# An attention kernel on TensorE: softmax sums over 8 rows with shared rows added by VectorE, outputs divided by GpSimd, fewer score columns, and layer 0's queries turned by VectorE

## The chip, the cores and the metric

The kernel runs on one core of a Trainium2 chip. The metric is the device time of one execution in microseconds (us). The five engines that matter are TensorE (PE; its weight loads are listed apart as PEld), VectorE (DVE), ScalarE (ACT), GpSimd (POOL) and SyncE (SP), which issues the transfers.

## The reference

The input `x` is 16 images of 64 x 64 positions with 256 channels, in float32. Two residual layers follow each other. Each starts with a group norm over 32 groups (`gn`, eps 1e-5, no scale or shift) and has 8 heads of 32.

```
# layer 0: linear attention over the n = 4096 positions of an image
q, k, v = split(gn(x) @ w_qkv)                # 8 heads x 32
q = softmax(q, over the 32 of a head) * 32**-0.5
k = softmax(k, over the 4096 positions)
context = einsum('bhdn,bhen->bhde', k, v)
x = x + einsum('bhde,bhdn->bhen', context, q) @ w_out

# layer 1: attention of each position to its 7 x 7 neighbours, zeros around the image
q, k, v = gn(x) @ Wq + bq, gn(x) @ Wk + bk, gn(x) @ Wv + bv
kp, vp = unfold(k, 7), unfold(v, 7)           # 49 neighbours of each position
kp = kp + e       # emb0 by row for heads 0 to 3, emb1 by column for heads 4 to 7
attn = softmax(einsum('bhwnd,bhwndk->bhwnk', q, kp), over the 49)
x = x + einsum('bhwndk,bhwnk->bhwnd', vp, attn)
```

## The kernel before

**Layout.** An image lies in SBUF as two tiles of 128 channels x 4096 positions, `img[k]`, each held twice, since the next image is loaded and normalised while the present one is worked on. The 4096 positions are in block order: 8 strips of 512, and a strip is a vertical stripe of 8 columns by 64 rows (strip 0 is made of the 3 columns at the left edge and the 5 at the right). `ORDER`, `KEYED` and `UNITS` are orders over strips and over units of the attention. `qq` (128 x 2 x 4096) holds layer 0's queries first and layer 1's later. PSUM has eight banks: `double` is two pairs (in the trace `pd`), `single` four banks (`ps`); `psum2()` takes the pairs by turns, `banks()` goes round all four pairs of banks.

**Order of the work.** For PE, ACT, DVE and SP the order of instructions is the order in which the code is written (`manual_schedule(engines=ORDERED)`); only POOL's is left to a scheduler. Semaphores make an engine wait for what it reads, and for the readers of a buffer that it overwrites. Everything runs image by image.

**Layer 0.** `layer0` has a loop of 16 steps of 256 positions. In a step, L524 makes queries and keys of two blocks of 128 positions on TensorE (positions on the partitions, 512 columns), L528 takes the exponential on ACT, L531 and L533 form the sums and reciprocals over a head on VectorE, L534 multiplies the queries by them on GpSimd. L542 adds the previous step's keys, times the input with a column of ones (257 columns), into two PSUM banks that stay open for the whole loop. `transposed` turns the queries of the step before that: four transposes by the identity on TensorE (L556) into one bank, and one copy of 512 columns into `qq`, by ACT in odd steps (L560) and by VectorE in even ones (L562). L284 normalises the strip that comes next. After the loop, `cc` holds the two halves of the normalised context, and `output_weights` (L302 to L324) turns them, multiplies them by the value weights, masks what belongs to other heads, and multiplies by `w_out`, into `w2`: one 256 x 256 matrix for the image. The output stage then takes, for each strip, four matmuls 128 x 128 x 512 of `w2` with `qq` (L602), and VectorE adds them to the image (L611) and takes the statistics for layer 1's group norm (L460).

**Layer 1, before the attention.** `positional` makes the scores of each query with the position embedding (L644, evacuated by L633 on ACT and L635 on VectorE), which go to DRAM and come back as 32 extra rows of `qq` (`store_rings`, `load_rings`); rows of masks stand beside the keys in `kaug` to match, so that one matmul of 64 rows gives key and embedding scores and a large negative number outside the 7 x 7. `values` (L692) makes the values and stores them padded to DRAM; `keys_queries` (L720) makes keys and queries for one half of the heads. The weights `wq`, `wk` and `wv` lie in SBUF as read, and are scaled into second tiles for each image.

**The attention.** `local_attention` runs twice per image, for half 0 (heads 0 to 3, `hg` = 0) and half 1. Each goes through four units of 16 columns of the image, each unit through 9 chunks `c` of 8 key rows, taken in five groups `g` of two (the last has one). The queries that see a chunk lie in the rows `lo` to `hi` of `span(c)`: 14 rows, or 8 at the top and 10 at the bottom. For each chunk and each of two planes `pl`:

- `scores` (L782): keys on the partitions, queries in the columns, into a pair of banks `pd`. The 128 partitions are two blocks `e` of 8 columns of keys. A block is reached by queries of 16 columns from up to three key strips, and the matmuls per row of queries take 10, 16 and 6 columns.
- ACT takes the exponential of all of them (L790) into a work tile `e`.
- `weighted` (L813), one group later (`held`): for each 8 columns `j` and each of 4 heads, one matmul with the values adds the weighted sum into `outs[j]`, and one with a matrix of ones adds the softmax's sum into `zs[j]`. All chunks of a unit add up in these four banks, which L800 fills with zeros first (`zb`, four matmuls with bf16 operands), since each adds only to the rows `lo` to `hi`.
- `finish`, after the last group of a unit: VectorE turns `zs` (L826), ACT copies `outs` out of PSUM (L827), VectorE copies the one column that matters, takes the reciprocal, turns it back to all rows (L831 to L833) and multiplies the outputs by it (L837); GpSimd adds them to the image (L846). The tiles for this come from a pool `tail` with two buffers.
- `between` puts other work between the groups: loads and statistics of the next image, its group norm, and the stores of what is done (`store_out`).

A matrix multiplication in float32 is recorded as two TensorE records for each instruction. A second, general path for inputs whose sums leave the safe range follows the fast one in the program; a flag `ok` skips it, and with these inputs it does not run.

## Time and profile before

| what | value |
|---|---|
| median of 3 runs | 5968.38 us (5966.06 to 5989.82) |
| profiled execution | 5964.21 us, of which the profile's span is 5962.4 us |
| mean granted TensorE clock in the span | 0.973 |
| busy share of the span | PE 92%, PEld 62%, DVE 49%, ACT 38%, POOL 17% |
| scores (L782) | 27648 records, 1012.9 us busy |
| products with values and with ones (L813) | 18432 records each, 841.1 and 839.4 us busy |
| exponentials (L790) | 1152, mean 839 ns |
| transposes of layer 0's queries (L556) | 1024 records, 151.0 us busy |
| transfers | 526.94 MB, 88 GB/s on average |

A row of the groups names the line, the engine, the operation, what it writes and reads (partitions x elements) and how often it ran; then the busy time and the mean of one in ns; then how long the engine was idle just before, and what ended most of that. In the table above a row can mix shapes; the shapes apart are shown where they are used. The chain of waits goes back from the last instruction, from each step to what released it or to the one before it on its engine; "issue" in it is time in which the engine waited for nothing that the profile shows.

### The profile page before, as it was taken

To read this page: it belongs to the slowest core of one execution; us is meant where nothing else is said; L and a number is where in the kernel's file an instruction comes from. 1 tells how busy PE (TensorE), PEld (TensorE's weight loads), DVE (VectorE), ACT (ScalarE), POOL (GpSimd) and SP (SyncE) were. 2 spreads that over 40 slices of the span, in tenths; PEclk is the share of its full clock that TensorE was granted. 3 is DMA by queue.
4 is the path that set the end of the run, shared out by engine and by line. 5 is a ranking of instruction groups with operands and counts; after the bars stand their busy time and mean duration, and the time that the engine had idled before them with its cause. 6 is when DMAs were issued, how large, how long until landed. Compare 5 with 4: busy or idle time off the path is not lost.

```text
span 5962.4 us, 171738 instructions
## 1 busy us (share of the span) xinstructions
PE 5478.6 (92%) x76913; PEld 3722.9 (62%) x76913; DVE 2892.6 (49%) x5034; ACT 2253.0 (38%) x3233; POOL 1029.1 (17%) x1944
## 2 busy tenths in 40 slices
PE   7999899998989989999899998999989999899998
PEld 4665666656666565665656656566565665656656
DVE  4544445554455544455445454444544545445454
ACT  1441523425244252442524425244252433515334
POOL 3021120211202012020121201212022120221202
PEclk9999999999999999999999999999999999999999
DMA  4543615435154361644516345073450724517244
GB/s 117 112 98 54 119 52 107 103 64 111 49 115 95 68 118 38 119 96 77 105 38 126 91 74 112 31 130 87 74 116 29 139 76 75 115 33 144 66 77 84
DMA packets 736939, 526.94 MB, mean 88 GB/s; under 512 B 240432, under 2 KB 667696, under 8 KB 733744
## 3 DMA queue, kind: packets, MB, share of 16 engines
q1 hardware_dynamic: 736192, 515.86, 42.6%
q8 instruction: 605, 9.91, 0.7%
q14 instruction: 142, 1.16, 0.1%
HBM read 357.02 MB, written 158.73 MB: 86 GB/s over the span
## 4 chain that ended last, share of the span: by engine, by line
PE 87%; ACT 4%; issue 4%; DVE 2%; SPq 1%; DMA 1%; POOL 1%; ACTq 0%; DVEq 0%; POOLq 0%
PE ps L813 16%; PE pd L782 15%; PE pd L524 14%; PE pd L720 7%; PE ps L542 7%; PE ps L720 6%; ACT qq L633 4%; PE ps L602 4%; PE pd L602 4%; PE ps L692 4%; PE pd L692 4%; PE ps L644 2%; PE ps L556 2%; PE ps L800 1%; SPq L504 0%
## 5 line engine op out<-in xcount | busy, mean ns | idle before, releaser
L790 ACT ACTIVATE e<-pd 128x896 f32<-128x896 f32 (+2 forms) x1152 | 924.2, 839 | 1039.7 <-PE pd L782 1037.8
L782 PE MATMUL pd<-qq,kaug 64*64 64x140 f32 (+5 forms) x27648 | 1012.9, 287 | 158.3 <-ACT qq L633 77.8
L782 PEld LDWEIGHTS pd<-qq,kaug 64*64 64x64 f32 x27648 | 891.3, 136 | 314.4 <-issue 170.6
L524 PE MATMUL pd<-wqkv,img 128*128 128x512 f32 x2048 | 922.2, 594 | 3.1 <-DVE img L284 3.1
L813 PE MATMUL ps<-e,ones 128*32 128x112 f32 (+1 forms) x18432 | 839.4, 253 | 65.2 <-issue 65.1
L813 PE MATMUL ps<-e,vw 128*32 128x112 f32 (+1 forms) x18432 | 841.1, 256 | 59.6 <-issue 59.2
L826 DVE STREAM_TRANSPOSE r<-ps 128x512 f32<-128x512 f32 x256 | 168.9, 697 | 1267.1 <-PE ps L813 1267.1
L438 POOL TENSOR_TENSOR others<-others,rc 128x16 f32<-128x16 f32 x256 | 113.5, 443 | 2961.3 <-DVE rc L831 2917.1
L528 ACT ACTIVATE eq<-pd 128x1024 f32<-128x1024 f32 x256 | 262.2, 1024 | 953.3 <-PE pd L524 953.3
L813 PEld LDWEIGHTS ps<-e,vw 128*32 128x32 f32 x18432 | 495.7, 111 | 202.8 <-issue 164.2
L633 ACT ACTIVATE qq<-ps,bias 32x512 f32<-32x512 f32 (+2 forms) x544 | 321.1, 623 | 781.0 <-PE ps L644 716.7
L524 PEld LDWEIGHTS pd<-wqkv,img 128*128 128x128 f32 x2048 | 372.4, 191 | 381.1 <-issue 352.4
L813 PEld LDWEIGHTS ps<-e,ones 128*32 128x32 f32 x18432 | 539.6, 112 | 76.4 <-issue 75.8
L531 DVE TENSOR_REDUCE qz<-eq 128x16 f32<-128x512 f32 x256 | 175.5, 686 | 829.2 <-ACT eq L528 829.2
L542 PE MATMUL ps<-xtok,eq 128*128 128x257 f32 x2048 | 486.1, 380 | 0.0
L542 PEld LDWEIGHTS ps<-xtok,eq 128*128 128x128 f32 x2048 | 386.1, 190 | 149.0 <-issue 107.1
L846 POOL TENSOR_TENSOR img<-img,r 128x320 f32<-128x320 f32 (+1 forms) x512 | 419.4, 840 | 165.3 <-DVE rc L831 164.1
L633 ACT ACTIVATE kaug<-pd,bias 32x512 f32<-32x512 f32 x256 | 173.9, 679 | 633.8 <-PE pd L720 630.9
L635 DVE TENSOR_SCALAR qq<-ps,bias 32x512 f32<-32x512 f32 x384 | 309.9, 807 | 146.8 <-PE ps L720 141.1
L460 DVE BATCH_NORM_STATS2 st<-img 128x6 f32<-128x512 f32 x512 | 334.9, 684 | 13.8 <-DMA img<-in_xc 5.1
L534 POOL TENSOR_TENSOR eq<-eq,qr 128x512 f32<-128x512 f32 x256 | 275.0, 1074 | 30.6 <-DVE qr L533 1.7
L720 PE MATMUL ps<-img,wqn 128*128 128x512 f32 x512 | 250.6, 635 | 0.0
(125 smaller groups left out, 6176.4 us busy)
## 6 DMA issues: line engine op xcount, KB each, us to landing
vw<-vpad SPq DMA_DIRECT2D x512, 288.0 KB
img<-in_xc SPq DMA_DIRECT2D x256, 256.0 KB
xtok<-in_xt SPq DMA_DIRECT2D x64, 1024.0 KB
out<-img SPq DMA_DIRECT2D x256, 256.0 KB
vpad<-v SPq DMA_DIRECT2D x112, 512.0 KB
qq<-pos SPq DMA_DIRECT2D x128, 256.0 KB
qq<-in_ring SPq DMA_DIRECT2D x128, 256.0 KB
pos<-qq SPq DMA_DIRECT2D x128, 112.0 KB
```

Of the source, the lines that this page charges most:

```text
L460: nc.vector.bn_stats(st[:, k, s], x[k][:, strip(s)])
L524: nc.tensor.matmul(ps[:, t], xn[k][:, n0 : n0 + P], n.wqkv_sb[:, k, : 2 * C], start=(k == 0), stop=(k == 1))
L542: nc.tensor.matmul(pc[hg][:, : C + 1], eq[p][:, t, C + hg * P : C + (hg + 1) * P], xtok[p // 4][:, 2 * (p % 4) + t], start=(p == 0 and t = ...
L602: nc.tensor.matmul(py[co], w2[:, hg, co * P : (co + 1) * P], qq[:, hg, strip(s)], start=(hg == 0), stop=(hg == 1),)
L633: nc.scalar.activation(dst, src, AF.Identity, bias=bias)
L635: nc.vector.tensor_scalar(dst, src, bias, None, ALU.add)
L692: nc.tensor.matmul(pi[:, t], x[k][:, n0 : n0 + P], wv[:, k], start=(k == 0), stop=(k == 1))
L720: nc.tensor.matmul(ps[a], wgt[:, k, hg * P : (hg + 1) * P], x[k][:, strip(pair[a])], start=(k == 0), stop=(k == 1),)
L782: nc.tensor.matmul(to, kaug[pl][rows, u, 8 * c : 8 * c + 8].rearrange("p r w -> p (r w)"), q, start=True, stop=True,)
L790: nc.scalar.activation(e, ps[:, :, : 2 * m], AF.Exp)
L813: nc.tensor.matmul(dst, ones if to is zs[j] else vw[:, j, c, h * HD : (h + 1) * HD], pr, start=False, stop=(c == NB - 1),)
L846: nc.gpsimd.tensor_tensor(yv, xv, by_rows(add[:, :, a - w0 : e - w0], xv), ALU.add)
```

## The change

1. **Queries of layer 0.** `transposed` becomes `turned`: two VectorE instructions per step transpose each 32 x 32 block of 128 x 256 within its partitions, straight from the work tile into `qq`. The queries lie differently then: partition 32a + d holds dimension d of every head, at the positions 32a to 32a + 31 of each block of 128. No transpose on TensorE and no copy is left.
2. **Output of layer 0.** To match, the output weights are kept per head on each of four groups of 32 rows (`w4`, in a buffer of the window pool). They are made by four transposes, 16 matmuls with 32 columns of weights, a scaling, eight matmuls with 32 rows, and three copies. The output stage takes, for two strips at a time, matmuls of 32 rows, 128 columns of weights and 256 columns of queries, adding over 8 heads, for four groups of rows `a`: 256 matmuls an image, where there were 32. VectorE adds the results to the image in 4 pieces of 256 for the first 128 channels and 2 of 512 for the second.
3. **Score columns.** The pieces of a row of 16 queries are 8, 14 and 6 columns instead of 10, 16 and 6. What is no longer written in `pd` is set to a large negative number once per half (`nb` times `bits`), and in half 1 the scores are laid out with a constant pitch of 16 rows so that these places stay the same for every chunk.
4. **Sums.** A row of queries reaches two chunks at 6 of 8 rows. `both_chunks` adds the 6 shared rows of the chunk before into this chunk's exponentials, in place, on VectorE. `summed` then multiplies by ones only the 8 rows that are complete after chunk `c`, for 16 columns at once, into their own columns of `zs`. The eight matmuls per chunk with ones (4 heads by two groups of 8 columns, over 14 rows) are replaced by four over 8 rows and 16 columns, or by eight over 6 and 2 rows where these lie on both sides of the border between the two banks of `zs`. The sums come one group after the products (`late`).
5. **Division.** `finish` is a generator of three parts, of which one runs per group. GpSimd multiplies the outputs by the turned reciprocals and then adds them to the image. The pool `tail` has one buffer for each of its two tags, `work` has six instead of four. The stores (`store_out`) are issued after the part with GpSimd.
6. **Weights.** `wq`, `wk` and `wv` have one tile each; SP loads them again for every image and VectorE scales them in place. `ORDER` changes so that pairs of strips stand together.

```diff
-ORDER = (3, 4, 5, 6, 7, 1, 2, 0)
+ORDER = (4, 5, 6, 7, 0, 1, 2, 3)
...
-        work = ctx.enter_context(tc.tile_pool(name="work", bufs=4))
-        tail = ctx.enter_context(tc.tile_pool(name="tail", bufs=2))
+        work = ctx.enter_context(tc.tile_pool(name="work", bufs=6))
+        tail = ctx.enter_context(tc.tile_pool(name="tail", bufs=1))
...
-            def transposed(p):
-                pt = other[p % 2]
+            def turned(p):
+
                 e = eq.pop(p)
...
+                for t in range(2):
+                    T = 2 * p + t
+                    nc.vector.transpose(qv[:, :, HD * T : HD * T + HD], e[:, t, :C].rearrange("p (h d) -> p h d", d=HD))
...
+            w4 = window(f"w4_{b}")[:, : 8 * C].rearrange("p (h g c) -> p h g c", h=4, g=2)
+            for h in range(2):
+                nc.vector.tensor_copy(w4[:, h].rearrange("p g c -> p (g c)"), double[0][:, h])
+            nc.scalar.copy(w4[:, 2:4].rearrange("p h g c -> p h (g c)"), double[1])
...
+            for i in range(NS // 2):
+                s0 = ORDER[2 * i]
...
                 for co in range(2):
...
+                    py = [double[a // 2][:, a % 2, : 2 * P] if co else single[a][:, : 2 * P] for a in range(4)]
+                    for h in range(4):
+                        for hg in range(2):
+                            for a in range(4):
+                                rows = slice(HD * a, HD * a + HD)
+                                nc.tensor.matmul(
+                                    py[a],
+                                    w4[rows, h, hg, co * P : (co + 1) * P],
+                                    qv[rows, 4 * hg + h, 8 * HD * i : 8 * HD * (i + 1)],
+                                    start=(h == 0 and hg == 0),
+                                    stop=(h == 3 and hg == 1),
+                                )
...
+        def load_weights(to, name):
+            nc.sync.dma_start(to, io[name].rearrange("(k p) f -> p k f", p=P))
...
-                    for e, u, w0, w1 in ((0, 2 * t, 0, 10), (1, 2 * t + 1, 0, 16), (0, 2 * t + 2, 10, 16)):
+                    for e, u, w0, w1 in ((0, 2 * t, 0, 8), (1, 2 * t + 1, 2, 16), (0, 2 * t + 2, 10, 16)):
...
+            def both_chunks(c, e, before):
+
+                r0 = 8 * c - 2 * PAD
+                part = rows_of(c, e, r0, 8 * c)
+                nc.vector.tensor_tensor(part, part, rows_of(c - 1, before, r0, 8 * c), ALU.add)
...
+            def summed(c, e):
...
+                r0, r1 = max(8 * c - 2 * PAD, 0), min(8 * c + 8 - 2 * PAD, W)
+                for i in range(2):
+                    a, z = max(r0, 32 * i), min(r1, 32 * i + 32)
+                    for h in range(4 if a < z else 0):
...
+                        nc.tensor.matmul(dst, ones, pr, start=True, stop=True)
...
+            def finish(i, t, r, pvs):
+
+                for k in range(2):
+
+
+                    nc.vector.transpose(r[:, k], zs[k])
+                yield
...
+                nc.vector.tensor_tensor(rc[:, 0], turned[:, :, 0], turned[:, :, 0], ALU.max)
+                nc.vector.reciprocal(rc[:, 1], rc[:, 0])
+                nc.vector.transpose(turned, rc[:, 1].unsqueeze(2).to_broadcast([P, 32, HD]))
+                yield
...
-                    nc.vector.tensor_tensor(pv, pv, r[j][:, 0], ALU.mult)
...
+                    nc.gpsimd.tensor_tensor(pv, pv, rz, ALU.mult)
...
+                stored(i)
+                yield
...
                 if held:
                     i, g, es = held
                     for c, e in es:
-                        weighted(UNITS[i], c, e, vw[i])
+                        weighted(c, e, vw[i])
                     if g == 4:
+                        rs[i] = [tail.tile([P, 2, 512], F32, tag=f"tail{k}", name=f"r{b}_{hg}_{i}_{k}") for k in range(2)]
+                        for j in range(2):
+                            nc.scalar.copy(rs[i][1][:, j], outs[j])
...
+                if late:
+                    i, g, es = late
+                    for c, e in es:
+                        summed(c, e)
+                    if g == 4:
+                        ends.append(finish(i, UNITS[i], *rs.pop(i)))
+                if held:
+                    for c, e in held[2]:
+                        if c:
+                            both_chunks(c, e, before)
+                        before = e
+                for end in list(ends):
+                    if next(end, True):
+                        ends.remove(end)
+                if late:
+                    between(*late[:2])
+                held, late = new, held
```

## The prediction

> **What bounds the kernel now.** I read the page from the top: busy shares, then the chain that ended last.

> ```profile
> PE 5478.6 (92%) x76913; PEld 3722.9 (62%) x76913; DVE 2892.6 (49%) x5034; ACT 2253.0 (38%) x3233; POOL 1029.1 (17%) x1944
> PE 87%; ACT 4%; issue 4%; DVE 2%; SPq 1%; DMA 1%; POOL 1%; ACTq 0%; DVEq 0%; POOLq 0%
> ```

> TensorE is 87% of the chain, so a tensor cycle removed is time unless something else takes its place. Taking each stage from the first record of its first line, an image (median of 16) is: queries and keys of layer 0 95.2 us, output of layer 0 33.1, positional 10.3, values 29.5, keys and queries 27.0, attention of half 0 73.5, keys and queries 26.5, attention of half 1 73.2. Both attentions are 40% of the span. Next the chain in order of time, inside an attention (start, us, what) and inside the loop of layer 0:

> ```profile
> 2478.95 1.68 PE pd L782 x37
> 2480.63 0.33 PE ps L800 x4
> 2480.95 1.36 PE ps L813 x64
> 2482.31 1.68 PE pd L782 x37
> 2483.99 1.28 PE ps L813 x47
> 2485.27 2.82 issue
> 2488.09 0.64 PE ps L813 x17
> ...
> 2338.36 3.44 PE pd L524 x8
> 2341.80 1.74 PE ps L542 x8
> 2343.54 0.44 PE ps L556 x4
> ```

> In attention scores (L782) and products (L813) alternate without a wait on ACT. Two chunks of 14 rows cost 1.68 us of scores and 1.67 of products; a unit of 9 chunks comes to 13.9 us. But units 1 and 2 of a half take 17.9 us from L800 to L800 on average: 4 us are lost. The "issue" piece is the largest part: TensorE stops in mid-group with no semaphore, and in the trace a 16 KB transfer of the instruction queue lands about 1 us before it resumes. Such gaps come to some 220 us over the run. The rest is half clock (mean granted clock 0.973).

> Then the groups by shape:

> ```profile
> L782 PE MATMUL pd<-qq,kaug 64*64 64x224 f32 x7168 | 833.7, 367 | 24.0 <-issue 24.0
> L813 PE MATMUL ps<-e,ones 128*32 128x112 f32 x14336 | 715.9, 265 | 62.0 <-issue 62.0
> L556 PE MATMUL ps<-ident,eq 128*128 128x128 f32 x1024 | 151.0, 273 | 0.0
> L800 PE MATMUL ps<-zb 32*128 32x512 bf16 x512 | 62.3, 384 | 48.2 <-ACT qq L633 48.1
> L837 DVE TENSOR_TENSOR r<-r 128x512 f32<-128x512 f32 x256 | 221.4, 865 | 28.2 <-DVE r L833 1.4 <-ACT eq L528 0.5
> L833 DVE STREAM_TRANSPOSE r<-rc 128x512 f32<-128x512 f32 x256 | 182.1, 711 | 8.8
> L534 POOL TENSOR_TENSOR eq<-eq,qr 128x512 f32<-128x512 f32 x256 | 275.0, 1074 | 30.6 <-DVE qr L533 1.7
> L846 POOL TENSOR_TENSOR img<-img,r 128x320 f32<-128x320 f32 x256 | 253.2, 989 | 165.3 <-DVE rc L831 164.1 <-DVE r L837 1.3
> L846 POOL TENSOR_TENSOR img<-img,r 128x192 f32<-128x192 f32 x256 | 177.0, 692 | 0.0
> ```

> The means of matmuls are latencies; their cost is the pitch. Start to start, the four column tiles of L813 take 42.6 ns a round at 48 columns and 56 at 64: 0.833 ns a column and 2.7 ns, per record. Each matmul is two records.

> [...] L837 takes 691 ns alone and up to 1256 when an L846 is running, starting its own work when that ends. [...] L800 is that shape: its four records start within 10 ns and the group costs 0.33 us, so here they do overlap, but in bf16 and one round only.

> **The change part by part**, against the profiled execution's 5964.2 us (span 5962.4 and 1.8 around it).

> 1. *Queries turned by VectorE.* L556 goes: 0.44 us in each of 16 steps of 16 images, less what the tail gives back. The tail from the last L542 to the first output matmul is now 6.8 us; the new one has the two cc steps 1.3, two scalings 0.9, 32 records in column tiles 1.0, a scaling 0.4, 16 row-tiled records 1.0, the first copy of w4 0.7 and handovers, some 6.5. Sum -110 us. Added on VectorE: two transposes of 256 a step. The 512 row is 711; half of it is the floor, 711 the ceiling; I take 0.43 each. With L531 0.69, L533 0.25 and L284 0.85 a step asks 2.65 us of VectorE under 5.17 of TensorE, so it is hidden (3.2 at the ceiling).

> 2. *Output of layer 0.* 32 matmuls of 512 columns become 256 of 256 with 32 rows, four abreast: 512 records, 128 rounds of 256 x 0.833 + 2.7 = 216 ns = 27.6 us against 28.0. Nothing, if they overlap. [...] The last evacuation grows from 0.70+0.69 to 2 x 0.69 + 2 x 0.68 = 2.75: +1.4 us on the path, +22. Its other VectorE work is 5.8 us per pair of strips under 6.9 of TensorE.

> 3. *Fewer score columns.* Each quadrant of the array streams 28 columns per row of queries instead of 32: 112 rows x 4 x 2 records x 0.833 = -0.75 us a unit, -96 over 128 units.

> 4. *Sums over 8 rows.* Before, 36 rounds of ones per unit: 28 x 96 + 4 x 56 + 4 x 43 = 3.08 us. After, 20: twelve of 128 columns at 109, four of 96 at 83, four of 32 at 29 = 1.76. -1.32 us a unit, -169. The score buffers' fill adds 0.33 a half, +11.

> 5. *Added waits.* The shared rows are added in place by VectorE, eight of 384 per unit at 0.56, or 0.4 behind a GpSimd instruction plus the wait for it. Each waits for the products that read the tile, and the sums, two steps behind the scores, wait for it; about 2.8 us of TensorE work lies between, so it is covered except at a half's last unit, where no scores follow: +0.8 us, +26. The multiply moves to GpSimd, and tail has one buffer per tag now: the ACT copy of a unit's outputs waits until GpSimd has finished the unit before. Behind that copy stand the next exponentials on ACT and the next unit's products on TensorE. The loop from copy to copy: two copies 1.2; next unit's first products, last sums, a group of scores and its products 3.5; VectorE's last addition, maximum, reciprocal (0.35 for 32) and transpose of 1024 (1.25) 2.6; GpSimd two multiplies 2.1 and adds 3.0 (half 1, where L846 runs at 1.15 and 0.74: 3.8); five additions of VectorE that exclude it 2.0: 14.4 us in half 0, 15.2 in half 1. TensorE's own unit is now 13.9 - 2.07 = 11.8, and with the 4 us lost today 15.8. So the loop is just covered while the losses stay outside it. Bounds for units 1 and 2 of each half: nothing, or losses fully on top of the loop, 15.0 + 4 - 15.8 = 3.2 us. I take 0.6: 64 x 0.6 = +38.

> 6. *At nothing:* SP gets four weight loads an image (0.9 MB of 33), needed a stage later; stores now wait on SP for GpSimd, and behind them stands a window load wanted one unit later. If that cover went, a late window stops products, as in 5. The end of the program gains a multiply, +2.

> Sum: -110 + 22 - 96 - 169 + 11 + 26 + 38 + 2 = -276: 5688, and since the median of the runs lies 4 us above the profiled execution, **5690**.

> **Rivals.** *The loop binds.* For it: 15 us is more than TensorE's 11.8, and instruction gaps fell 6 us after a unit's end, where the loop's TensorE part lies. [...] Losses on top: (3.2 - 0.6) x 64 = +166: 5856. *Row tiles don't overlap* (the slower side): if the 128-column weights of the four row tiles load one after another at L556's 110 ns, a record costs 110 instead of 54 ns: 512 x 56 = +28.7 us an image, +459: about 6150. It decides above 89 ns a record (276/16/512 = 34 ns more than 54). For it: nothing here shows fp32 weights in this shape. Against: loads of L813 for four column tiles start 7 ns apart at a round of 42.6, and L800. *Fewer records, fewer gaps:* part 5's 64 us and some 30 of the gaps vanish: 5595. *That it does not do what it says* is excluded by the instruction order: L556 is gone and the products lose 4096 matmuls.

> **Numbers.** Forecast with its better case 0.65, loop 0.22, row tiles 0.10, about even 0.03. A measurement of this kernel can tell 0.5% (30 us) from no change. Range 5590 (better case) to 5860 (loop). Faster 0.87, same 0.03, slower 0.10.

> **What would show it.** Right: L524 and L542 alternate with nothing between; output stage of 28 us plus 2.75; pairs of chunks at 1.49 us for scores; units 1 and 2 near 16 us with the ACT copy waiting for GpSimd less than 1 us. Wrong: output stage above 40 us; that copy waiting over 2 us a unit, or VectorE's additions followed by idle TensorE in every group; gaps in the instruction stream growing though records fall.

## The result, and the profile after

The changed kernel takes 5882.4 us (median of 4 runs, 5872.7 to 5892.4) against 5968.1: a ratio of 0.985 (95% interval 0.982 to 0.988), some 90 us faster. The forecast was 5690, with a range of 5590 to 5860. The direction was right, and two thirds of the gain are missing. In what follows a ratio is always to the kernel before, run on the same chip, and 0.001 is 6 us.

The page of the changed kernel, busy shares and then the chain of waits by engine:

```profile
PE 5235.4 (89%) x75313; PEld 3609.8 (61%) x75313; DVE 3439.0 (58%) x5946; ACT 2193.7 (37%) x3089; POOL 1335.2 (23%) x1946
...
PE 77%; DVE 8%; ACT 5%; issue 5%; DMA 2%; SPq 1%; POOL 1%; DVEq 0%; ACTq 0%; POOLq 0%
```

TensorE's share of the chain fell from 87% to 77%, VectorE's rose from 2% to 8%. The mean clock fell too, from 0.973 to 0.954: 546 us at half clock instead of 327. By stage, from the first record of its first line, summed over the 16 images (us; the last two columns are the experiments e5 and e2 below):

| stage | before | after | layer 0 alone | ends by TensorE |
|---|---|---|---|---|
| queries and keys of layer 0 | 1529 | 1458 | 1438 | 1434 |
| output of layer 0 | 545 | 574 | 583 | 571 |
| positional | 166 | 187 | 189 | 188 |
| values | 473 | 473 | 471 | 471 |
| keys and queries, both halves | 856 | 877 | 815 | 867 |
| attention of half 0 | 1190 | 1103 | 1190 | 1085 |
| attention of half 1 | 1172 | 1182 | 1212 | 1117 |

By the prediction's sum, half 1 should have become 95 us shorter; it became 10 us longer. Groups of the changed kernel by shape; after the bar stand busy time and mean, then the idle time ahead of the group and what ended it:

```profile
L834 PE MATMUL pd<-qq,kaug 64*64 64x196 f32 x7168 | 755.9, 345 | 19.1 <-issue 18.8
L863 DVE TENSOR_TENSOR e<-e,e 128x384 f32<-128x384 f32 x1024 | 732.4, 742 | 773.1 <-PE ps L878 615.2 <-ACT e L843 73.0 <-ACT e L846 61.6
L878 PE MATMUL ps<-e,vw 128*32 128x112 f32 x14336 | 492.5, 273 | 63.5 <-issue 62.9
L908 PE MATMUL ps<-e,ones 128*32 128x128 f32 x6144 | 307.9, 290 | 108.2 <-DVE e L863 86.1 <-issue 20.6
L934 POOL TENSOR_TENSOR r<-r,r 128x512 f32<-128x512 f32 x256 | 340.7, 1352 | 140.5 <-DVE r L921 134.8 <-ACT e L846 5.8
L970 ACT COPY r<-ps 128x512 f32<-128x512 f32 x256 | 137.2, 591 | 151.7 <-POOL xtok L460 77.5 <-POOL img L942 37.1 <-PE ps L908 31.4
```

The sums (L908) wait for VectorE's additions (L863), which take 742 ns on average. The 653 that run with no L934 or L942 of GpSimd's beside them take 557 (median), the 0.56 us that was the author's estimate; the slowest of the 371 others takes 1645. Where the GpSimd instruction was running first, the addition ends 0.41 us after it (median of 352), as taken, and L837 of the kernel before ends 0.54 to 0.55 us after an L846 in all 127 such pairs. GpSimd is held up in turn: an L934 takes 1.27 us with no addition beside it and 1.59 when one was running first (medians of 121 and 70). And ACT's copy (L970) does wait for GpSimd, 115 us in all, as the loop of the prediction's first rival says. Where the first of these waits lies, the chain in order of time shows at the end of a half 1 (start, us, what):

```profile
2579.88 0.70 PE ps L878 x21
...
2581.96 0.03 issue
2581.99 0.02 DVEq L863
2582.01 0.09 issue
2582.10 0.02 DVEq L915
2582.12 0.17 issue
2582.29 1.31 DVE img L285
2583.60 2.34 DVE e L863 x2
2585.94 1.33 DVE img L285 x2
2587.27 0.48 DVE e L863
2587.74 0.04 issue
2587.79 0.55 PE ps L908 x8
2588.33 9.11 PE pd L531 x16
```

TensorE stands still for over 5 us while VectorE normalises two strips of the next image (L285) between the three additions that the last sums need, two of which take 2.34 us beside GpSimd. Then layer 0 starts at half clock: 16 records in 9.11 us, where 7.06 is usual. The idle time ahead of L908 in the last unit comes to 31 us in the 16 halves 0 and 73 us in the 16 halves 1 (42 and 88 from the start of one record to the start of the next).

The clock recorded in these traces is full or half: a 128x512 record of L531 starts 429 ns after the one before at full clock and 854 at half (medians). In the trace of the changed kernel all pieces at half clock but the last are multiples of 3.41 us. Cut into windows of 3.41 us that start with the clock's own changes, it has 56 windows at full clock in which TensorE's records fill less than 40%. All 56 are followed by half clock, and only two of them are wholly idle. Of the 1401 windows that are filled to 60% or more, two are followed by it. The kernel before gives the same picture, with 47 of 47 and 0 of 1500. So stops of some 2 us in a window (60% of 3.41, an estimate from these windows), as there are many inside the attention, can cost clock as well.

### The profile page after: what moved, and what is told of

It reads as the page before. It is cut to its first block, busy times and chain, and to the rows that moved or that the text cites. A ratio compares the mean times of both kernels' runs of the same rounds, so it can differ in the third digit from the quotient of the medians.

```text
span 5890.5 us, 169110 instructions
## 1 busy us (share of the span) xinstructions
PE 5235.4 (89%) x75313; PEld 3609.8 (61%) x75313; DVE 3439.0 (58%) x5946; ACT 2193.7 (37%) x3089; POOL 1335.2 (23%) x1946
## 4 chain that ended last, share of the span: by engine, by line
PE 77%; DVE 8%; ACT 5%; issue 5%; DMA 2%; SPq 1%; POOL 1%; DVEq 0%; ACTq 0%; POOLq 0%
PE pd L531 15%; PE pd L834 13%; PE ps L878 8%; PE pd L771 7%; PE ps L549 6%; PE ps L771 5%; ACT qq L684 4%; PE ps L642 4%; PE pd L743 4%; PE pd L642 4%; PE ps L743 4%; PE ps L908 4%; DVE e L863 3%; PE ps L695 2%; DMA vpad<-v 1%
## 5 line engine op out<-in xcount | busy, mean ns | idle before, releaser
L863 DVE TENSOR_TENSOR e<-e,e 128x384 f32<-128x384 f32 x1024 | 732.4, 742 | 773.1 <-PE ps L878 615.2
L834 PE MATMUL pd<-qq,kaug 64*64 64x112 f32 (+4 forms) x27648 | 938.0, 277 | 159.8 <-issue 71.1
L834 PEld LDWEIGHTS pd<-qq,kaug 64*64 64x64 f32 x27648 | 813.2, 139 | 319.5 <-issue 181.8
L531 PE MATMUL pd<-wqkv,img 128*128 128x512 f32 x2048 | 948.8, 608 | 3.2 <-DVE img L285 3.2
L531 PEld LDWEIGHTS pd<-wqkv,img 128*128 128x128 f32 x2048 | 399.1, 196 | 412.1 <-issue 376.6
L878 PE MATMUL ps<-e,vw 128*32 128x112 f32 (+1 forms) x18432 | 575.2, 261 | 65.2 <-issue 64.5
L846 ACT ACTIVATE e<-pd 128x896 f32<-128x896 f32 (+2 forms) x576 | 461.4, 836 | 430.5 <-PE pd L834 423.5
L908 PE MATMUL ps<-e,ones 128*32 128x128 f32 (+2 forms) x10240 | 404.2, 266 | 146.3 <-DVE e L863 113.0
L878 PEld LDWEIGHTS ps<-e,vw 128*32 128x32 f32 x18432 | 419.0, 114 | 154.4 <-issue 117.5
L942 POOL TENSOR_TENSOR img<-img,r 128x320 f32<-128x320 f32 (+1 forms) x512 | 493.2, 993 | 0.0
L549 PE MATMUL ps<-xtok,eq 128*128 128x257 f32 x2048 | 483.4, 380 | 0.0
L549 PEld LDWEIGHTS ps<-xtok,eq 128*128 128x128 f32 x2048 | 387.4, 190 | 149.8 <-issue 107.1
L686 DVE TENSOR_SCALAR qq<-ps,bias 32x512 f32<-32x512 f32 (+2 forms) x416 | 312.3, 759 | 151.0 <-PE ps L771 145.2
L934 POOL TENSOR_TENSOR r<-r,r 128x512 f32<-128x512 f32 x256 | 340.7, 1352 | 140.5 <-DVE r L921 134.8
L908 PEld LDWEIGHTS ps<-e,ones 128*32 128x32 f32 x10240 | 253.3, 116 | 189.6 <-DVE e L863 148.1
```

Of the source, the lines that this page charges most:

```text
L531: nc.tensor.matmul(ps[:, t], xn[k][:, n0 : n0 + P], n.wqkv_sb[:, k, : 2 * C], start=(k == 0), stop=(k == 1))
L549: nc.tensor.matmul(pc[hg][:, : C + 1], eq[p][:, t, C + hg * P : C + (hg + 1) * P], xtok[p // 4][:, 2 * (p % 4) + t], start=(p == 0 and t = ...
L834: nc.tensor.matmul(to, kaug[pl][rows, u, 8 * c : 8 * c + 8].rearrange("p r w -> p (r w)"), q, start=True, stop=True,)
L863: nc.vector.tensor_tensor(part, part, rows_of(c - 1, before, r0, 8 * c), ALU.add)
L878: nc.tensor.matmul(dst, stationary, pr, **flags)
L908: nc.tensor.matmul(dst, ones, pr, start=True, stop=True)
```

## The experiments

| run | ratio to before (95%) | us to before |
|---|---|---|
| the change | 0.985 (0.982 to 0.988) | -91 |
| e1, no additions | 0.957 (0.953 to 0.960) | -258 |
| e2, ends of halves by TensorE | 0.968 (0.965 to 0.972) | -191 |
| e4, division by VectorE | 0.987 (0.984 to 0.991) | -76 |
| e7, all shared rows by TensorE | 0.989 (0.986 to 0.992) | -67 |
| e9, e2 with the group norm first | 0.970 (0.966 to 0.974) | -180 |
| e5, layer 0 alone | 0.996 (0.995 to 0.998) | -23 |
| e6, columns alone | 0.999 (0.997 to 1.000) | -8 |
| e16, the change with the old columns | 0.989 (0.985 to 0.992) | -69 |
| e10, before, fewer window loads | 0.969 (0.966 to 0.972) | -186 |
| e11, e10 with fewer columns | 0.971 (0.968 to 0.974) | -172 |
| e14, e11 with half the columns | 0.967 (0.965 to 0.969) | -198 |
| e15, e11 with fewer instructions | 0.948 (0.945 to 0.950) | -311 |
| e12, before, loads spread | 1.001 (0.999 to 1.002) | +3 |
| e13, e2, loads spread | 0.983 (0.980 to 0.985) | -104 |

### The additions, or the loop over GpSimd?

**e1.** In the changed kernel:

```diff
-                        if c:
-                            both_chunks(c, e, before)
```

> The changed kernel (5882 us) without the VectorE additions of shared rows: 1024 instructions of 742 ns are left out, and with them part of the softmax sums. Theory V (TensorE waits for these additions, above all after the last products of a half, and then runs at half clock): the 122 us of waits of the sums at the ends of halves go, some 40 us of such waits elsewhere, and about half of the extra 218 us at half clock, so 5690 us (5640 to 5750), with a mean clock of 0.97 or more. Theory L (the ACT copy of a unit's outputs waits for GpSimd, because there is one buffer): only the exclusion of GpSimd by the additions goes, 2 us of a loop of 15; at most 60 us gained, 5820 us or more, and the copy still waits about 0.9 us a unit for GpSimd.

The ratio is 0.957, 168 us below the change, as theory V has it, though the mean clock (0.964) stayed under the 0.97 that V expected. The copy's wait for GpSimd fell with it, to 28 us, so this run's time alone doesn't exclude the loop. What TensorE waits for speaks against it: in the change it waits 2.3 us in all for that copy, and 59 us for exponentials, which stand behind the copy on ACT. In e1, where the copy hardly waits, the exponentials cost it the same 59 us.

**e2.** In the last two groups of a half, TensorE multiplies ones with the shared rows of the chunk before as well, into the same PSUM columns:

```diff
-                        summed(c, e)
+                        last = at_end(i, g)          # i == 3 and g >= 3
+                        summed(c, e, last or None)   # with last: not the end of the accumulation
+                        if last:
+                            summed(c, tiles[c - 1], None, c - 1)
...
-                        if c:
+                        if c and not at_end(*held[:2]):
                             both_chunks(c, e, before)
```

> The changed kernel with the shared rows of the last three chunks of each half (chunks 6, 7 and 8 of the fourth unit) added by TensorE in PSUM (four more matmuls of 96 columns with ones for each chunk) instead of by VectorE. Theory V: the end of a half waits for nothing any more: 122 us less, 16 us more on TensorE (96 times 0.17), and the half clock after the ends of halves goes too (some 50 us): 5730 us (5700 to 5780). Theory L: the loop over GpSimd lies inside a half, and nothing follows its end: no change, 5880 us.

The ratio is 0.968, 100 us below the change, and nothing is left out: of the versions that compute everything this is the fastest, ahead of both kernels (e9 below cannot be told from it). Theory L allowed nothing. The chain of e2 at the same place:

```profile
2542.94 0.90 PE ps L878 x32
2543.85 0.45 PE ps L910 x23
2544.30 0.17 PE ps L878 x16
2544.47 0.60 PE ps L910 x17
2545.07 0.43 issue
2545.50 0.92 PE ps L910 x27
2546.42 7.06 PE pd L531 x16
```

Sums (L910 here) follow products without VectorE, and layer 0 starts at full clock. The queries' stage loses 24 us by that, though nothing in it was changed; time at half clock falls from 546 to 411 us. ACT's copy waits even longer for GpSimd (137 us), and the kernel is faster all the same: the loop is not what binds.

**e4.** The division back on VectorE:

```diff
-                    nc.gpsimd.tensor_tensor(pv, pv, rz, ALU.mult)
+                    nc.vector.tensor_tensor(pv, pv, rz, ALU.mult)
```

> The changed kernel with the multiplication by the reciprocals back on VectorE (256 instructions, 1352 ns each on GpSimd now, 690 to 870 ns on VectorE). Theory V: VectorE gets 1.5 us more per unit and loses about as much of what GpSimd's exclusion adds to it (the additions fall from 742 towards 650 ns); little changes, 5890 us (5850 to 5940). Theory L: the loop through GpSimd becomes 1.2 us or more shorter in each unit after which a copy waits: 5805 us, and the copy's wait for GpSimd goes below 0.3 us a unit.

The two groups of VectorE in e4, additions and multiplication:

```profile
L863 DVE TENSOR_TENSOR e<-e,e 128x384 f32<-128x384 f32 x1024 | 632.2, 645 | 778.9 <-PE ps L878 617.6 <-ACT e L846 71.6 <-ACT e L843 67.0
L934 DVE TENSOR_TENSOR r<-r,r 128x512 f32<-128x512 f32 x256 | 164.7, 685 | 3.3
```

There is no difference that can be told from the change (the intervals overlap). VectorE gets 165 us of multiplications and its additions become 100 us shorter (645 ns). Who divides does not matter. As a test of the loop the run is weak: the copy still waits 94 us for GpSimd instead of 115, where theory L had expected under 0.3 us a unit.

**e7.** All shared rows by TensorE, one group earlier (`summed(c, e, of)` takes the rows of chunk `c` from chunk `of`):

```diff
-                if late:
-                    i, g, es = late
-                    for c, e in es:
-                        summed(c, e)
...
                     for c, e in held[2]:
+                        summed(c, e, c)
                         if c:
-                            both_chunks(c, e, before)
+                            summed(c, before, c - 1)
                         before = e
```

> The changed kernel with all shared rows added by TensorE in PSUM: no VectorE addition at all, eight times 0.17 us more of matmuls a unit, and the sums one group earlier (in the step of their products). The output is the full one. Theory V: +171 us of matmuls, against 160 us of waits and some 100 us of half clock saved: 5790 us (5740 to 5850). Theory L: TensorE's extra work is hidden behind the loop, the loop itself loses the five additions that exclude GpSimd: 5850 to 5880 us. If neither wait counts, 5882 + 171 = 6050 us.

The ratio is 0.989; 5790 was expected and 5897 measured, so the expectation missed: it took off 260 us for waits and half clock, where leaving the additions out altogether (e1) had brought 168. Against e1, which does not sum the shared rows at all, the extra matmuls cost 0.032, 190 us. With ones TensorE streams as many columns here, in as many records (18432), as in the kernel before. So part 4 with its additions is worth some 24 us, with overlapping intervals: without it the kernel is only that much slower.

**e9.** In e2, the group-norm steps of the next image ahead of the additions:

```diff
+                ahead = bool(late) and hg == 1 and late[0] == 2 and late[1] < 3
+                if ahead:
+                    between(*late[:2])
                 if held:
                     for c, e in held[2]:
...
-                if late:
+                if late and not ahead:
                     between(*late[:2])
```

> The run with the last three chunks of a half summed by TensorE (5771 us), and in addition the three steps of the next image's group norm (third unit of half 1) are put ahead of that group's additions in VectorE's order. Theory V, in the form that any VectorE instruction which TensorE waits for suffers from standing behind the additions: the third unit of half 1 takes 18.5 us and should take 16 (that of the run without additions), 2.5 x 16 = 40 us less, 5731 us (5715 to 5750). If that unit is long for another reason (the loop over GpSimd, whose copy still waits 137 us in that run): no change, 5771 us.

There is no change (0.970 against 0.968), and that unit is 19.2 us long instead of 18.5. Why it takes 16.0 in e1 and 18.5 in e2 stays open.

### The parts by themselves

**e5.** The changed kernel with the whole of `local_attention` as before, and its pools:

```diff
-        work = ctx.enter_context(tc.tile_pool(name="work", bufs=6))
-        tail = ctx.enter_context(tc.tile_pool(name="tail", bufs=1))
+        work = ctx.enter_context(tc.tile_pool(name="work", bufs=4))
+        tail = ctx.enter_context(tc.tile_pool(name="tail", bufs=2))
```

> Parts 1, 2 and 6 alone: the changed kernel with the attention of the kernel before (products, sums, score columns and division as they were). The prediction's working: -110 + 22 = -88 us, 5875 us. From the trace of the changed kernel: its queries' stage takes 71 us less, its output 29 and its positional stage 21 more, but some 25 us of the first are half clock that comes from the end of the attention and should be absent here: -96 + 28 + 21 = -47 us, 5915 us (5900 to 5930).

The run is 23 us faster than the kernel before (13 to 32), about half of what was expected. The stage table says where (its two profiled executions are 33 us apart): queries -91, output +38, positional +23. Attention and its keys and queries together are unchanged. The positional stage had been costed at nothing: with the new `ORDER` the strip made of two narrow pieces is evacuated by VectorE instead of ACT, and the bias of the values stands behind it there. In the trace of the change, TensorE waits 17 us for that bias (L1039), in every second image.

**e6.** The kernel before with the new pieces, the fill and the pitch of 16 rows:

```diff
-for e, u, w0, w1 in ((0, 2 * t, 0, 10), (1, 2 * t + 1, 0, 16), (0, 2 * t + 2, 10, 16)):
+for e, u, w0, w1 in ((0, 2 * t, 0, 8), (1, 2 * t + 1, 2, 16), (0, 2 * t + 2, 10, 16)):
```

> Part 3 alone: the kernel before with score pieces of 8, 14 and 6 columns, the fill of the score buffers once per half and the constant pitch in half 1. The prediction's working: -96 + 11 = -85 us, 5875 us. If the time that TensorE loses in the middle of groups (some 220 us, with no semaphore) grows as the matmuls shorten, because the number of instructions stays the same, half of it comes back: about 5920 us.

The run is 8 us faster (0 to 16), less than either expectation. The chain in an attention of that run:

```profile
2496.09 1.50 PE pd L786 x38
2497.58 0.46 PE ps L809 x4
2498.04 1.35 PE ps L822 x64
2499.39 1.50 PE pd L786 x37
2500.89 0.32 PE ps L822 x5
2501.20 1.60 issue
2502.80 1.72 PE ps L822 x59
```

The scores of two chunks do take 1.50 us instead of 1.68, as worked out. TensorE's stops without a semaphore ("issue") in scores and products do not shrink with them: they come to 207 us, against 197 before. Time at half clock rises from 327 to 391 us, which at half speed is worth some 32 us.

**e16** puts the old pieces back into the changed kernel. Theory C has TensorE bound by the columns that it streams, theory S by the supply of instructions:

> The changed kernel with the score pieces of 10, 16 and 6 columns as before. It has 192 records per pair of chunks instead of 224. Theory C: 0.75 us a unit, 85 to 96 us more than 5882: 5970 us. Theory S: part of that, since 192 records in 2.84 us is 3.79 us per 256 and thus less near the supply's limit: 5920 us (5890 to 5950).

The ratio is 0.989 against 0.985: about 20 us with overlapping intervals, at the low end of what S allowed and far from the 85 of C.

### What the columns ran into

In the trace of the kernel before, the stop that the prediction shows (2485.27 to 2488.09) has this history: instruction transfers of 16 KB, each good for 256 records of matmuls and weight loads (e15 below has 16384 records and 64 transfers fewer than e14), start at 2471.0, 2474.8 and 2478.6, and the next only at 2485.4. From 2480 to 2486 a window load moves some 200 KB a us in packets of 512 bytes. Of the 221 us of gaps in the attentions that end just after an instruction transfer, 192 follow such packets. An interval between two such transfers has a median of 5.2 us when these packets move in it and of 3.8 when they don't. **e10** tests it:

```diff
-                        vw.pop(i)
                         if i + 2 < 4:
-                            vw[i + 2] = load_window(b, hg, UNITS[i + 2])
+                            vw[i + 2] = vw.pop(i)
```

> The kernel before, without the loads of the values' windows for the third and fourth unit of each half (they use the windows of the first and second again, so the output is not the reference's). Theory F: TensorE's gaps in mid-group come from the instruction transfer that has to wait behind a window load[...] (192 of the 221 us of such gaps follow one); some 150 us of them lie in the two units in which these loads run, and go: 5815 us (5780 to 5850). Rival, the gaps depend on the amount of instructions alone: no change, 5960 us.

The run is 186 us faster; the gaps fall from 116 with 221 us to 55 with 70, and time at half clock from 327 to 222 us. The chain in an attention of e10, where groups run without a stop:

```profile
2498.33 1.68 PE pd L782 x37
2500.01 0.33 PE ps L800 x4
2500.34 1.35 PE ps L813 x64
2501.69 1.68 PE pd L782 x37
2503.37 1.77 PE ps L813 x62
2505.15 1.68 PE pd L782 x38
2506.83 1.67 PE ps L813 x64
```

**e11.** The same edit in e6, and so with its columns.

> The same kernel (no window loads for the third and fourth unit) with part 3, the fewer score columns. Theory F: a unit in which a window is loaded is as long as the instruction transfer makes it, however short its matmuls; without the loads, fewer columns give nearly what the prediction said: 70 to 85 us less than the run without part 3, 5735 us. Rival, TensorE's time in the scores does not go with columns, or the fill and the pitch cost what the columns save: the same 5 us as with the loads, 5810 us.

The ratio is 0.971 against 0.969. With the loads gone, fewer columns still bring nothing: F explains the large gaps but not this. Time at half clock is 270 us against 222 in e10. Two more runs keep the window loads out. **e14** streams 14 columns instead of the 28 of e11, with as many instructions:

```diff
-((0, 2 * t, 0, 8), (1, 2 * t + 1, 2, 16), (0, 2 * t + 2, 10, 16))
+((0, 2 * t, 0, 4), (1, 2 * t + 1, 2, 9), (0, 2 * t + 2, 10, 13))
```

> The kernel before without the window loads of the third and fourth units, with 14 score columns for each row of queries and quadrant instead of 28 (pieces of 4, 7 and 3; the places left out hold a constant, so the output is not the reference's), and with just as many instructions. Theory C (TensorE is bound by the columns): 14 columns in 112 rows, twice the records, are 2.6 us a unit, 128 units: 335 us less than the 5792 us of the run with 28, so 5460 us. Theory S (bound by the supply of instructions, at least 3.35 us per 256 records, where a clean pair of chunks with 28 columns already takes 3.61): at most 60 us less, 5735 us (5690 to 5790).

The run is 26 us below e11, with intervals that overlap, where theory C wanted 335. The chain in an attention of e14:

```profile
2497.60 1.35 PE ps L822 x64
2498.95 0.49 PE pd L786 x16
2499.44 0.35 issue
2499.79 0.78 PE pd L786 x21
2500.58 1.67 PE ps L822 x64
2502.25 0.82 PE pd L786 x28
2503.07 0.48 issue
2503.54 0.48 PE pd L786 x8
2504.03 1.67 PE ps L822 x64
```

A clean pair of chunks, one without a stop, has scores of 1.06 us here instead of 1.50. Over all units that is an estimate of 220 us (0.43 us for each of four pairs in 128 units), so C's 335 was too much even for clean groups. Most of the 220 does not arrive: TensorE's idle time in the attentions is 97 us more than in e11, and time at half clock 83 us more, worth 41. **e15** joins the matmuls with ones to 16 columns: 192 records in a pair of chunks instead of 224, as many columns.

```diff
+                for i in range(2):
+                    a, z = max(lo, 32 * i), min(hi, 32 * i + 32)
+                    for h in range(4 if a < z else 0):
...
+                            pr = pr[:, 16 * (a - lo) : 16 * (z - lo)]
...
+                        nc.tensor.matmul(dst, ones, pr, start=False, stop=last)
                 for j in range(2):
-                    for to in (outs[j], zs[j]):
+                    for to in (outs[j],):
```

> The kernel before without the window loads of the third and fourth units and with 28 score columns (5792 us), and the matmuls with ones joined to 16 columns: four per chunk instead of eight, 32 fewer records of 224 per pair of chunks, and just as many columns streamed (the division then uses sums in another order, so the output is not the reference's). Theory S: fewer instructions for the same columns let the 28 columns count: 60 to 85 us less, 5720 us. Theory C: no change, 5790 us.

The run is 139 us below e11, twice what S expected. The joined matmuls are not faster in themselves: a clean pair of chunks takes 3.16 us, as in e11, and time at half clock is the same (269 us against 270). The instruction transfers over the whole run (number, MB, share of the DMA engines), of e14 and then of e15:

```profile
q8 instruction: 605, 9.91, 0.7%
```
```profile
q8 instruction: 541, 8.86, 0.7%
```

64 transfers fewer are worth 2.2 us each. The table has the time from one instruction transfer to the next inside attentions (the value that 1% fall below, and the median, in us) and the gaps that end after one (number, us):

| run | clean time of 256 records | interval, 1% | median | gaps, us |
|---|---|---|---|---|
| before | 3.83 | 3.35 | 4.05 | 116, 221 |
| e10 | 3.83 | 3.34 | 3.80 | 55, 70 |
| e11 | 3.61 | 3.32 | 3.81 | 81, 96 |
| e14 | 3.12 | 3.31 | 3.79 | 169, 196 |
| e15 | 4.21 | 3.36 | 4.03 | 29, 42 |

(Clean: the shortest pair of chunks of 14 rows, 3.35, 3.16 and 2.73 us for 224 records and 3.16 for 192. A unit's last chunk is reached by 6 rows of queries, not by the 10 named at the start.) However short the matmuls, the median interval stays at 3.8 us, four at most of some 460 are below 3.3, and none is below 3.2. The pairs show the same. The median of 113 pairs of 14 rows is 3.35 us in e10, 3.57 in e11 and 3.41 in e14, all with 224 records, and 3.16 in e15 with 192. In these runs, where 256 records of clean matmuls would take less than some 3.8 us, the supply of instructions sets the pace, and columns count only where they take longer.

**e12** and **e13** cut each window load into its four transfers, one per group, in the kernel before and in e2:

```diff
+                    if g < 4 and todo:
+                        nc.sync.dma_start(*todo.pop(0))
...
-                            vw[i + 2] = load_window(b, hg, UNITS[i + 2])
+                            vw[i + 2] = load_window(b, hg, UNITS[i + 2], True)   # fills todo
```

> The kernel before with each window load inside an attention cut into its four transfers of 288 KB, one issued per group of the following unit, instead of all four at its start (the full output). Theory F: an instruction transfer waits behind at most one piece, some 1.5 us[...]: 100 us less, 5860 us (5810 to 5910). Rival, gaps follow the amount of instructions or of bytes: 5960 us.

> The changed kernel with the last three chunks of a half summed by TensorE (5771 us) and window loads spread in the same way. Theory F: the same gaps (173 us after window loads in that run) shrink by about 100 us: 5670 us (5620 to 5720). Rival: 5770 us.

Neither gained. In e12 the gaps moved (110 with 196 us). One piece seems to delay an instruction transfer as well as the whole does: intervals with such packets in them have a median of 5.4 us there. e13 lost 87 us against e2: the window comes late, and products wait for it, as the group of e13 says:

```profile
L883 PE MATMUL ps<-e,vw 128*32 128x112 f32 (+1 forms) x18432 | 581.6, 263 | 128.5 <-DMA vw<-vpad 102.0 <-issue 26.4
```

## Why the prediction was wrong, step by step

Two terms of the sum failed most. The additions of part 5 were put at +26 and cost 168, and the columns of part 3 were put at -85 and brought 8 to 20. Layer 0 was put at -88 and brought 23.

- **Part 1, -110.** Measured -91 in e5. Two of the 16 steps' transposes stood in the tail, which the sum had costed separately; 14 x 0.44 x 16 is 99. The new tail was right (6.5 us from the start of the last L549 to the first output matmul), but the old one takes 6.5 us as well on the mean of 16 images, not 6.8, so it gave nothing back. A transpose on VectorE takes 0.39 us (0.43 was taken), and it was hidden.
- **Part 2, +22.** The row tiles overlap, as taken: 64 records of the output stage in 3.45 us, 54 ns each. The rival of 6150 us was wrong. The stage is 29 us longer in the change and 38 in e5, and the part beyond 22 is about what half clock costs: it covers 63 us of the stage in the change and 91 in e5, against 48 before.
- **Weights and order, "at nothing".** The positional stage became 21 us longer in the change and 23 in e5. The new strip order sends more evacuations to VectorE, and the prediction did not follow it to the engine that evacuates.
- **Part 3, -96 + 11.** This step failed: -8 alone, about -20 in the change. Its price, 0.833 ns a column, is right for a clean group (1.49 us of scores, as named). But it was taken as the stage's price, though the profile had shown "issue" pieces of 220 us there. The prediction left those as a constant. They do not shrink with the matmuls: 197 us before and 207 in e6, 64 in e10, 83 in e11 and 177 in e14. With them grows the time at half clock (327 us before and 391 in e6, 222 in e10, 270 in e11, 353 in e14), which had no term either.
- **Part 4, -169.** The size is about right: 190 between e7 and e1. Columns and records both fall there (by 171 us of columns at the prediction's price, and by 16384 records of matmuls and weight loads), so this pair does not say which of them paid. e15, which drops as many records and no columns, gives 139.
- **Part 5, the additions +26.** This step failed too, as a term far too small: e1 puts them at 168 us, 100 of which e2 recovers at the ends of halves. The prediction priced the additions at 0.56, the author's estimate, and "+0.8 us" at a half's end; they took 0.74 on average, stood behind the next image's statistics and normalisation in VectorE's order, and TensorE idled some 2 us in the last unit of a half 0 and 4.5 us in that of a half 1. After that came the half clock, on which the sum had no term.
- **The loop, +38, and its rival (5856).** The loop's pieces on VectorE are as taken (reciprocal of 32 0.353 us, transpose of 1024 1.245); GpSimd's multiplication takes 1.27 us with no addition beside it, where half of 2.1 was taken. The rival's number is near the measured time by luck: the copy waits 115 us for GpSimd as described, but e2 gains with that wait at 137, and TensorE itself waits only 2.3 us for the copy.
- **"Fewer records, fewer gaps" (5595)** had the right cause and was given as a bonus on top of the columns. The stops without a semaphore did shrink by the 30 us that it names, from 197 to 167 us (L834, L878 and L908). More did not go, since the change's shorter groups use instructions faster than before: a clean pair of 192 records in 2.68 us is 256 in 3.57 us, against 3.83.

Together: -23 for layer 0, -8 for the columns and a rest of -60 for all of parts 4 and 5 make the -91. The predicted -276 had -88, -85 and -103 for them.

What is shown and what not: that TensorE waited for the additions at the ends of halves is shown by e1 and e2. That the number of instructions and not that of score columns sets the attention's pace is shown by e14 and e15, with half of the window loads left out. That window loads hold up instruction transfers is shown by e10 and the intervals. Why two transfers hardly come closer than 3.3 us is not shown, nor how much of what the columns did not bring is half clock that the stops cause.

## What to carry to other kernels

Where TensorE runs many small matmuls, count instructions before columns (here half the score columns changed the time by 26 us, with overlapping intervals, and 8192 matmuls fewer by 139): compare the time of 256 records in a clean stretch with the interval of the instruction transfers (3.8 us here), and treat "issue" in mid-group as a limit rather than as noise. Work moved to another engine is cheap only while something stands between it and its reader; at the end of a stage, where nothing does, let the reader's own engine do it (e2), which brought 100 us here, and count the half clock that follows where TensorE is idle for much of a 3.41 us window (here after all 56 that it filled to less than 40%).
